# Expert rows gathered up to sixteen blocks ahead, row and result stores on ScalarE's queue, and a second product two blocks behind, in a two-layer mixer with routed experts

## The chip, the core and the metric

The kernel runs on one core of a Trainium2 chip. The metric is the device time of one execution in microseconds; the median of three runs of the kernel before is 674.62 us (672.95 to 680.81). Durations below come from one execution that was profiled. In the profile, PE is TensorE's matmul, PEld its weight load, DVE is VectorE, ACT is ScalarE, POOL is GpSimd and SP is SyncE; an instruction is named by its line in the kernel (L543), and tiles by the program's names.

## What is computed

The input x has 8 sequences of 256 tokens with 128 channels. Two layers follow each other, each a token mixer and a feed-forward part with eight experts of width 512, of which each token uses two:

```python
x = x + ga * mixer(layernorm(x) * (1 + ca) + sa)
x = x + gb * experts(layernorm(x) * (1 + cb) + sb)
```

The vectors sa, ca, ga, sb, cb, gb come from a small modulation product for each sequence. Layer 0's mixer is a retention with 16 heads of 8 channels, a decay mask, a normalisation for each head and a gate; layer 1's is softmax attention with a causal mask inside chunks of 256. The experts are `relu(x W1 + b1) W2 + b2` in layer 0 and `(silu(x G) * (x U)) D` in layer 1; each token's two experts are the two largest router logits, weighted by a softmax over these two.

## The kernel before

**Tiling.** The 2048 tokens are four groups of 512 (two sequences each), and a half is two groups, 1024 tokens. The mixers work through groups and sequences; the experts work through halves.

**Experts as sorted rows.** `route` (L382) makes the router logits of a half, takes the two best experts of each token, and gives each of the 2048 (token, expert) pairs a slot so that each expert's slots form whole blocks of 128. A half has NS = 23 blocks. The modulated tokens (tile hm, made by POOL) are stored to DRAM as xs (L401). A product of one-hot tiles (hot, L512) with owner tiles, the matmul pown (L520), gives the token list: token number for each slot (L529).

`gather` (L535, DMA at L543) brings the 128 rows of one block from xs into one quarter of a row tile xr; a row tile holds NTL = 4 blocks, and there are three. `begun` (L548) issues the first eight gathers of the first half of a layer and reports after the fourth that the layer can begin. `experts` (L556) loops over the 23 blocks: `matrices` (L574) has SP read the block's expert number and load its weights (six buffers); `hidden0` or `hidden1` makes the first product from xT, the transposed rows (`turn`, L563); `leave` (L588) makes the second product py (L591) of the block before, copies it to yr, and `store` (L599) sends four blocks at a time to ys in DRAM on ACT's queue. `combined` (L634) then gathers both results of each token from ys (yk, L659), weights and adds them, and adds them to x with `add_gated` (L346), on POOL except for the last half. In layer 1 the finished x is stored to the output (L1192).

**Order.** The order on each engine is the order in which the program writes the instructions; nothing is reordered. Work that isn't in the loop at hand is written as generators, the side jobs, kept in a list. `tick` (L171) moves each of them by one step, `ticks(step)` does so several times at a place in a loop, and `hop(step)` inside a job makes it pause for several ticks. PACE (L41) gives these numbers, 1 where a step isn't named. `settle` (L186) runs side jobs to their end with no loop beside them. The stages are: retention with the routing of layer 0 beside it, until the first gathers are written (L1173); experts of half 0 and of half 1 of layer 0, with layer 1's modulation, the combination of half 0 and the opening of the attention beside them (`Attention.opening`, L1100); attention with the routing of layer 1; experts of both halves of layer 1, with the combination of half 0 beside the second; the combination of half 1 alone at the end (L1197).

**Queues.** Gathers of both kinds, row stores (L401) and half 0's output stores are DMAs on POOL's queue, between POOL's own work (rstd, hm, masks, placing, adding x). Weights go on SP's queue, ys stores on ACT's.

Of the kernel before, what the change touches and what calls it, by code (L numbers as in the profile page):

```python
# [10 lines left out]
FP = mybir.dt.float32  # L11
BF = mybir.dt.bfloat16
# [6 lines left out]
P = 128  # L19
# [13 lines left out]
W0 = 2 * FF + NFC  # L33
NSC = 7
# [6 lines left out]
PACE = {  # L41
    "a0.kt": 3, "a0.rstd": 3, "a0.xn": 2, "a1.k": 2, "a1.q": 2, "a1.rstd": 2, "a1.stats": 2,
    "a1.turn": 2, "a1.xn": 0, "att.sums": 2, "att.weights": 0, "c0.b2": 2, "c0.begin": 2,
    "c0.gw": 3, "c1.begin": 8, "c1.gather": 0, "c1.scale": 4, "cl.begin": 3, "cl.pp": 0,
    "head3": 0, "n.pp": 0, "n.q": 2, "n.rstd": 2, "op.max": 2, "op.place": 0, "r0.both": 2,
    "r0.rstd": 4, "r1.rstd": 2, "ret.scores": 2, "ret.sums": 2,
}
# [3 lines left out]
def kernel(  # L51
# [239 lines left out]
    def modulated_norm(key, g, layer, shift, scale, got, hm=None):  # L291


        st = sm.tile([P, NTL, 6], FP, tag="lnst", name=f"lnst_{key}")
# [87 lines left out]
    def route(layer, half, ready, wr, bias):  # L382
# [10 lines left out]
        for u in range(HG):  # L393
            g = HG * half + u
            while g not in ready:
# [5 lines left out]
            nc.gpsimd.dma_start(  # L401
                out=xs[half].rearrange("(u t p) c -> u p t c", p=P, t=NTL)[u], in_=hm
            )
# [7 lines left out]
            yield from hop(f"r{layer}.logits")  # L411
            if bias is None:
                nc.vector.tensor_copy(lg[:, tiles, :], pv)
            else:
                nc.vector.tensor_tensor(
                    lg[:, tiles, :], pv, bias.unsqueeze(1).to_broadcast([P, NTL, NE]), ALU.add
                )
# [4 lines left out]
        at = sm.tile([P, 2, HT], FP, tag="at", name=f"at_{key}")  # L422
# [33 lines left out]
        need = sm.tile([P, NE], FP, tag="need", name=f"need_{key}")  # L456
        nc.vector.tensor_reduce(need, big, AX.X, ALU.add)
        nc.vector.tensor_tensor(big, upto, need.unsqueeze(1).to_broadcast([P, NE, NE]), ALU.mult)
        ends = sm.tile([P, NE], FP, tag="ends", name=f"ends_{key}")
        nc.vector.tensor_reduce(ends, big, AX.X, ALU.add)  # L460
        first = sm.tile([P, NE], FP, tag="first", name=f"first_{key}")
# [11 lines left out]
        slot_f = sm.tile([P, 2, HT], FP, tag="slf", name=f"slf_{key}")  # L473
# [4 lines left out]
        row = sm.tile([P, 2, HT], I32, tag="row", name=f"row_{key}")  # L478
# [29 lines left out]
        for t in range(HT + 2):  # L508
            if t < HT:
                for k in range(2):  # L510
                    hot = sm.tile([P, P], BF, tag="hot", name=f"hot_{key}_{k}_{t}", bufs=8)
                    nc.vector.tensor_scalar(  # L512
                        hot, row16, part[:, 1, k, t : t + 1], None, ALU.is_equal
                    )
                    hots.append(hot)
# [17 lines left out]
    raw, begin = {}, set()  # L533

    def gather(layer, half, j):  # L535

        q, t = j // NTL, j % NTL
        if t == 0:
            raw[layer, half, q] = wk.tile(
                [P, NTL, P], FP, tag="xr", name=f"xr_{layer}_{half}_{q}", bufs=3  # L540
            )
        token = routed[layer, half][4]
        nc.gpsimd.indirect_dma_start(  # L543
# [12 lines left out]
    def experts(layer, half, blob, hidden, following=None):  # L556
# [48 lines left out]
        last = None  # L605
        ahead = [(layer, half, j) for j in range(2 * NTL, NS)]
        if following:
            ahead += [(*following, j) for j in range(2 * NTL)]
        total = len(ahead)
        for j in range(NS):  # L610
            q = j // NTL
            for _ in range(2):
                if ahead and ahead[0][:2] in routed and total - len(ahead) <= j:
                    gather(*ahead.pop(0))
# [6 lines left out]
            if last is not None:  # L621
                leave(*last)
# [3 lines left out]
            last = (j, w2, h, yr)  # L626
        leave(*last)
# [6 lines left out]
    def combined(layer, half, finished, add=nc.gpsimd):  # L634
# [16 lines left out]
        for at in range(HT + 2):  # L651
# [43 lines left out]
            add_gated(f"{key}_{u}", g, gates, 1, acc, acc, add)  # L695
            finished(g)
# [19 lines left out]
    def retention(groups, finished):  # L716
# [93 lines left out]
        def normed(g, n):  # L810
# [4 lines left out]
            if n == 0:  # L815
                gn[g] = (
                    sm.tile([P, 2, 6], FP, tag="gnst", name=f"gnst_{key}"),
# [94 lines left out]
    class Attention:  # L912
# [58 lines left out]
        def maxima(self, at, c, k):  # L971
# [29 lines left out]
            if k == c:  # L1001
# [6 lines left out]
                rest = sm.tile([P, 4, 4], FP, tag="nrest", name=f"nr_{tag}")  # L1008
# [151 lines left out]
    with tc.manual_schedule():  # L1160
# [34 lines left out]
        sides.append(combined(1, 0, leaves(nc.gpsimd)))  # L1195
# [101 lines left out]
```

## Time and profile before

| | us |
|---|---|
| median of three runs | 674.62 |
| the profiled execution, whole | 674.16 |
| its span, first to last instruction | 672.5 |
| PE busy | 522.9 (78%) |
| DVE busy | 359.7 (53%) |
| POOL busy | 326.0 (48%) |
| ACT busy | 234.5 (35%) |
| row gathers, L543, 92 of them | 88.5, mean 0.962 |
| result gathers, L659, 64 of them | 61.5, mean 0.960 |

From the timelines, the stages begin and end at about these times: retention until 121, experts of layer 0 from 134 to 205 and from 206 to 296, attention from 299 to 479, experts of layer 1 from 483 to 566 and from 568 to 641, the last combination until 672.

Busy is time in which an engine works on an instruction of its own; waiting for a semaphore and issuing DMAs are not in it, except that a GpSimd DMA's row counts the time in which POOL makes the DMA. "Idle before" is the time an engine stood before the instructions of a group, and the name after the arrow is what ended most of it; "issue" stands for time in which the profile shows nothing that was waited for. A matmul in float32 shows as two records. The granted clock is TensorE's, as a share of full speed.

### The profile page before, as it was taken

The page shows a single profiled execution, that of the slowest core. Times are in us where ns is not written, and L with a number is a line of the kernel's source. Part 1 is how long each engine was busy: PE and PEld are TensorE (multiplying, and loading weights), DVE is VectorE, ACT ScalarE, POOL GpSimd, SP SyncE. Part 2 cuts the span into 40 slices and gives each one's busy share as a digit, 9 for nine tenths or more (in the row PEclk, how much of TensorE's full clock was granted, in tenths as well). Part 3 has the DMA queues.
Part 4 walks back from the last instruction along what each step waited for, and adds up shares of the span by engine and source line. Part 5 has one row for each costly group of instructions (what it writes and reads, how often), then busy time and mean ns, then how long its engine had stood idle before and what let it go on. Part 6 is the DMA issues. An engine that isn't in the chain of part 4 may idle for free.

```text
span 672.5 us, 13020 instructions
## 1 busy us (share of the span) xinstructions
PE 522.9 (78%) x4672; PEld 400.6 (60%) x4672; DVE 359.7 (53%) x1137; ACT 234.5 (35%) x517; POOL 326.0 (48%) x458
## 2 busy tenths in 40 slices
PE   4798885596778588987888888588797799889910
PEld 4555453386777487663454444345697798789910
DVE  3668879374533245646588667956153632223422
ACT  2453442233123244364555545234423122123310
POOL 4466682676243435317667427146446042613364
PEclk9999796799777799998799999979899899899965
DMA  6000002458666257500100000010698699689412
GB/s 185 25 1 1 18 1 86 151 169 204 212 203 207 94 182 204 182 28 18 31 18 17 2 1 17 7 39 21 195 342 196 244 280 315 227 281 311 170 58 63
DMA packets 43087, 84.13 MB, mean 125 GB/s; under 512 B 6472, under 2 KB 21456, under 8 KB 43024
## 3 DMA queue, kind: packets, MB, share of 16 engines
q1 hardware_dynamic: 25072, 64.42, 28.3%
q0 software_dynamic: 5792, 12.86, 8.6%
q10 hardware_dynamic: 12160, 6.03, 3.0%
q8 instruction: 37, 0.61, 0.4%
q14 instruction: 26, 0.21, 0.1%
HBM read 74.11 MB, written 9.18 MB: 124 GB/s over the span
## 4 chain that ended last, share of the span: by engine, by line
PE 36%; DVE 12%; issue 8%; POOL 5%; ACT 3%; another core or an unknown queue 2%; DMA 1%; POOLq 0%; ACTq 0%; DVEq 0%
PE py L591 7%; PE pg L1150 5%; DVE nm L995 5%; PE pu L1150 4%; PE sm L989 4%; PE ph L892 3%; POOL yk_c L659 3%; PE se L1042 2%; PE sm L981 2%; PE yd L1067 1%; PE pn L1084 1%; DMA yk_c<-ys,slot_r 1%; PE pz L1020 1%; ACT e L1048 1%
## 5 line engine op out<-in xcount | busy, mean ns | idle before, releaser
L543 POOL DMA_INDIRECT xr<-xs,token_r x92 | 88.5, 962 | 92.9 <-PE pt_s L281 26.3
L659 POOL DMA_INDIRECT yk_c<-ys,slot_r x64 | 61.5, 960 | 55.1 <-issue 35.7
L995 DVE TENSOR_REDUCE nm<-sm 128x4 f32<-128x512 f32 x96 | 59.5, 681 | 39.2 <-PE sm L989 39.2
L1157 DVE TENSOR_TENSOR h<-pu,sg 128x512 f32<-128x512 f32 x46 | 31.7, 690 | 88.8 <-PE pu L1150 46.6
L1048 ACT ACTIVATE e<-se 128x512 f32<-128x512 f32 x96 | 49.7, 603 | 47.4 <-PE se L1042 37.0
L892 PE MATMUL ph<-xT,we 128*128 128x128 f32 x368 | 55.7, 299 | 10.9 <-ACT xT L569 9.3
L591 PE MATMUL py<-we,h 128*128 128x128 f32 x368 | 54.4, 293 | 7.4 <-issue 5.0
L359 POOL TENSOR_SCALAR_AFFINE_SELECT e<-e 128x512 f32<-128x512 f32 x64 | 38.4, 633 | 43.2 <-ACT e L1048 43.0
L892 PEld LDWEIGHTS ph<-xT,we 128*128 128x128 f32 x368 | 50.9, 213 | 11.3 <-ACT xT L569 10.1
L1150 PE MATMUL pg<-xT,we 128*128 128x128 f32 x368 | 52.6, 287 | 6.3 <-ACT xT L569 4.3
L591 PEld LDWEIGHTS py<-we,h 128*128 128x128 f32 x368 | 49.5, 206 | 12.1 <-issue 7.0
L1155 ACT ACTIVATE sg<-pg 128x512 f32<-128x512 f32 x46 | 27.4, 597 | 81.4 <-PE pg L1150 54.7
L591 PE MATMUL py<-wd,h 128*128 128x128 f32 x368 | 50.3, 278 | 3.8 <-issue 2.0
L1150 PE MATMUL pu<-xT,we 128*128 128x128 f32 x368 | 50.3, 279 | 3.7 <-issue 3.7
L900 DVE TENSOR_SCALAR h<-ph,we 128x128 f32<-128x128 f32 x92 | 27.9, 344 | 47.1 <-PE ph L892 20.6
L1150 PEld LDWEIGHTS pg<-xT,we 128*128 128x128 f32 x368 | 47.5, 201 | 8.8 <-ACT xT L569 4.8
L898 ACT ACTIVATE h<-ph,we 128x128 f32<-128x128 f32 x92 | 28.7, 364 | 60.9 <-issue 29.2
L1150 PEld LDWEIGHTS pu<-xT,we 128*128 128x128 f32 x368 | 46.8, 197 | 3.8 <-issue 3.8
L591 PEld LDWEIGHTS py<-wd,h 128*128 128x128 f32 x368 | 44.9, 192 | 4.5 <-DVE h L1157 2.4
L595 DVE COPY yr<-py 128x128 f32<-128x128 f32 x92 | 26.4, 287 | 34.4 <-PE py L591 12.2
L989 PE MATMUL sm<-kz,qs_a 32*128 32x512 f32 x192 | 34.3, 721 | 0.0
L569 ACT COPY xT<-pt_s 128x512 f32<-128x512 f32 (+1 forms) x24 | 13.6, 567 | 55.6 <-PE pt_s L281 42.6
(221 smaller groups left out, 982.6 us busy)
## 6 DMA issues: line engine op xcount, KB each, us to landing
we<-in_l_ew_dram SPq DMA_DIRECT2D x46, 514.0 KB
we<-in_l_ew_dram SPq DMA_DIRECT2D x46, 512.0 KB
wd<-in_l_ew_dram SPq DMA_DIRECT2D x46, 256.0 KB
ys<-yr ACTq DMA_DIRECT2D x20, 256.0 KB
xs<-hm_r POOLq DMA_DIRECT2D x8, 256.0 KB
xr<-xs,token_r POOLq DMA_INDIRECT x92
x<-in_x_in_dram SPq DMA_DIRECT2D x4, 256.0 KB
yk_c<-ys,slot_r POOLq DMA_INDIRECT x64
```

What stands on the lines that cost most here:

```text
L359: nc.gpsimd.affine_select(out=src, in_=src, compare_op=ALU.is_ge, fill=0.0, base=0, pattern=[[0, 4], [1, P]], channel_multiplier=-1,)
L543: nc.gpsimd.indirect_dma_start(out=raw[layer, half, q][:, t, :], out_offset=None, in_=xs[half][:, :], in_offset=bass.IndirectOffsetOnAxis( ...
L591: nc.tensor.matmul(py, lhsT=h[:, fc, :], rhs=w2[:, fc * C : (fc + 1) * C], start=(fc == 0), stop=(fc == NFC - 1),)
L659: nc.gpsimd.indirect_dma_start(out=yk[:, k, :], out_offset=None, in_=ys[half][:, :], in_offset=bass.IndirectOffsetOnAxis(ap=slot[:, k, at ...
L892: nc.tensor.matmul(ph[:, i, :], lhsT=we[:, fc * P : (fc + 1) * P], rhs=xT, start=True, stop=True)
L898: nc.scalar.activation(h[:, fc, :], ph[:, i, :], AF.Relu, bias=b1)
L900: nc.vector.tensor_scalar(h[:, fc, :], ph[:, i, :], b1, 0.0, ALU.add, ALU.max)
L989: nc.tensor.matmul(scs[i], lhsT=qs[part, t0 : t0 + P], rhs=kz[part, :, k * P : (k + 1) * P], start=(k != c), stop=True,)
L995: nc.vector.tensor_reduce(nm[:, 4 * i : 4 * i + 4], scs[i], AX.X, ALU.max, negate=True)
L1048: nc.scalar.activation(e, scs[i], AF.Exp)
L1150: nc.tensor.matmul(p[:, fc, :], lhsT=we[:, i * FF + fc * P : i * FF + (fc + 1) * P], rhs=xT, start=True, stop=True,)
L1157: nc.vector.tensor_tensor(h, pu, sg, ALU.mult)
```

## The change

Six things are changed.

- Gathers: `experts` writes up to two gathers for each block, one ahead of the first product and one after the second product. A rule on row tiles replaces the count: a gather is written if its row tile is less than four row tiles ahead of the one in use. There are four row tiles xr in place of three, and 16 blocks of the following half are gathered in the loop of the half before, in place of 8. `begun` still writes eight.
- The row store of xs moves from POOL's queue, ahead of the logits, to ACT's, after the pause at the logits.
- The output stores of half 0 move from POOL's queue to ACT's, and a pause named c1.out stands ahead of them.
- With e1.behind at 2, layer 1's second product is written two blocks behind the first.
- PACE has other numbers for a good part of the steps.
- Small tiles have fewer buffers (3 to 2, hot 8 to 4).

```diff
+AHEAD = 16
 PACE = {
-    "a0.kt": 3, "a0.rstd": 3, "a0.xn": 2, "a1.k": 2, "a1.q": 2, "a1.rstd": 2, "a1.stats": 2,
-    "a1.turn": 2, "a1.xn": 0, "att.sums": 2, "att.weights": 0, "c0.b2": 2, "c0.begin": 2,
-    "c0.gw": 3, "c1.begin": 8, "c1.gather": 0, "c1.scale": 4, "cl.begin": 3, "cl.pp": 0,
-    "head3": 0, "n.pp": 0, "n.q": 2, "n.rstd": 2, "op.max": 2, "op.place": 0, "r0.both": 2,
-    "r0.rstd": 4, "r1.rstd": 2, "ret.scores": 2, "ret.sums": 2,
+    "a0.kt": 3, "a0.rstd": 3, "a0.xn": 2, "a1.hT": 2, "a1.k": 2, "a1.q": 3, "a1.rstd": 2,
+    "a1.stats": 0, "a1.turn": 2, "a1.xn": 0, "att.sums": 2, "att.weights": 0, "blanks": 2,
+    "c0.begin": 2, "c0.gw": 3, "c1.begin": 8, "c1.gather": 2, "c1.out": 3, "c1.scale": 2,
+    "cl.begin": 4, "cl.pp": 0, "e1.behind": 2, "head10": 0, "head13": 2, "head3": 0, "head9": 0,
+    "mod.rows": 2, "n.pp": 0, "n.q": 2, "n.rstd": 2, "op.first": 4, "op.max": 3, "op.place": 0,
+    "op.project": 0, "r0.count": 0, "r0.hot": 0, "r0.logits": 0, "r0.rstd": 4, "r0.top": 0,
+    "r0.xn": 0, "r1.count": 0, "r1.logits": 0, "r1.rstd": 4, "ret.scores": 2, "ret.sums": 2,
 }
...
-            nc.gpsimd.dma_start(
-                out=xs[half].rearrange("(u t p) c -> u p t c", p=P, t=NTL)[u], in_=hm
-            )
...
             yield from hop(f"r{layer}.logits")
+            nc.scalar.dma_start(
+                out=xs[half].rearrange("(u t p) c -> u p t c", p=P, t=NTL)[u], in_=hm
+            )
...
-                    hot = sm.tile([P, P], BF, tag="hot", name=f"hot_{key}_{k}_{t}", bufs=8)
+                    hot = sm.tile([P, P], BF, tag="hot", name=f"hot_{key}_{k}_{t}", bufs=4)
...
-                [P, NTL, P], FP, tag="xr", name=f"xr_{layer}_{half}_{q}", bufs=3
+                [P, NTL, P], FP, tag="xr", name=f"xr_{layer}_{half}_{q}", bufs=AHEAD // NTL
             )
         token = routed[layer, half][4]
+        gathered[layer, half] = j + 1
...
-        last = None
-        ahead = [(layer, half, j) for j in range(2 * NTL, NS)]
+        hiddens = []
+        ahead = [(layer, half, j) for j in range(gathered[layer, half], NS)]
         if following:
-            ahead += [(*following, j) for j in range(2 * NTL)]
-        total = len(ahead)
+            ahead += [(*following, j) for j in range(AHEAD)]
+
+        def onward(j):
+
+            if ahead and ahead[0][:2] in routed:
+                part, at = ahead[0][1:]
+                if at // NTL + (part - half) * -(-NS // NTL) < j // NTL + AHEAD // NTL:
+                    gather(*ahead.pop(0))
+
         for j in range(NS):
             q = j // NTL
-            for _ in range(2):
-                if ahead and ahead[0][:2] in routed and total - len(ahead) <= j:
-                    gather(*ahead.pop(0))
+            onward(j)
...
             store()
-            if last is not None:
-                leave(*last)
+            if len(hiddens) == PACE.get(f"e{layer}.behind", 1):
+                leave(*hiddens.pop(0))
+            onward(j)
             ticks(f"e{layer}.leave")
...
-            last = (j, w2, h, yr)
-        leave(*last)
+            hiddens.append((j, w2, h, yr))
+        for more in hiddens:
+            leave(*more)
         store()
...
             add_gated(f"{key}_{u}", g, gates, 1, acc, acc, add)
+            if layer == 1:
+                yield from hop("c1.out")
             finished(g)
...
-        sides.append(combined(1, 0, leaves(nc.gpsimd)))
+        sides.append(combined(1, 0, leaves(nc.scalar)))
```

## The prediction

> **What bounds it now.** I read the slices of the page first, then windows around every hole of TensorE, then the timelines of the engines in the holes, then the groups of the lines that the diff touches. The slices (16.8 us each) of the page:
>
> ```profile
> PE   4798885596778588987888888588797799889910
> DVE  3668879374533245646588667956153632223422
> POOL 4466682676243435317667427146446042613364
> ```
>
> TensorE (PE) is busy 78% of the span. No engine is full throughout, so what counts is TensorE's holes: the hand-over from layer 0's mixer to its experts (slice 7), holes inside the expert loops, and the tail (the last two slices). The windows of three of these (columns: length, then busy us and count of PE, weight loads, DVE, ACT, POOL, then granted clock, DMA share, GB/s):
>
> ```profile
> 96.00:122.00 26.00, 17.89 (x206) 11.26 (x206) 21.19 (x91) 7.28 (x15) 10.85 (x17) 0.74 0.35 118
> 126.00:134.00 8.00, 2.45 (x11) 1.29 (x11) 0.00 (x0) 0.58 (x1) 6.65 (x9) 0.58 0.26 66
> 212.00:231.00 19.00, 11.31 (x66) 10.40 (x65) 6.44 (x18) 3.98 (x13) 11.48 (x12) 0.77 0.32 99
> ```
>
> VectorE (DVE) limits the end of the mixer, 21.2 of 26 us, and then does nothing for 8 us. Why, the two timelines say:
>
> ```profile
> 121.75 0.18 DVE L529 SCALAR_TENSOR_TENSOR token_r<-pown_r,low_r 128x23 int32<-128x23 f32 x1
> ...
> 136.08 0.61 DVE L900 TENSOR_SCALAR h<-ph,we 128x128 f32<-128x128 f32 x2 [10.12 <-PE ph L892]
> ```
> ```profile
> 129.59 0.48 PE L281 MATMUL pt_s<-ident,xr 128*128 128x128 f32 x1 [2.38 <-DMA xr<-xs,token_r]
> 131.90 0.48 PE L281 MATMUL pt_s<-ident,xr 128*128 128x128 f32 x1 [1.83 <-DMA xr<-xs,token_r]
> 132.82 0.48 PE L281 MATMUL pt_s<-ident,xr 128*128 128x128 f32 x1 [0.44 <-DMA xr<-xs,token_r]
> 133.97 0.58 PE L892 MATMUL ph<-xT,we 128*128 128x128 f32 x1 [0.68 <-ACT xT L569]
> ```
>
> The token list is ready at 121.9, four gathers follow, and the first expert matmul runs at 134.0. These four gathers are the only ones TensorE ever waits for; so more rows ahead, by itself, removes no wait of TensorE. In layer 1 the token list (447.4) comes 35 us before the first expert matmul (482.7), so nothing is to be had there. The tail, on GpSimd (POOL):
>
> ```profile
> 642.34 1.25 POOL L355 TENSOR_TENSOR x<-x,acc_c 128x512 f32<-128x512 f32 x1 [10.52 <-DVE acc_c L352]
> 643.89 0.81 POOL L1192 DMA_DIRECT2D out_dram<-x  x1 [0.29 <-POOL x L355]
> 645.00 0.99 POOL L659 DMA_INDIRECT yk_c<-ys,slot_r  x1 [0.30 <-issue]
> ```
>
> Sixteen such gathers, 1.25 us apart, carry the last 27 us, and a store stands ahead of them. The gathers' group on the page, and what the second product waits for (view of L591, 482 to 641):
>
> ```profile
> L543 POOL DMA_INDIRECT xr<-xs,token_r x92 | 88.5, 962 | 92.9 <-PE pt_s L281 26.3
> ```
> ```profile
>   DVE h L1157: 4.2, 6
> ```
>
> **The skill.** The Trainium skill, "DMA: Bandwidth & Descriptors", section "Issuing engines are not separate DMA queues", says that the issuing engine changes only the sequencer time spent on the issue. The trace bears this out as far as it shows: a 256 KB store keeps POOL 0.81 to 0.86 us (plus 0.3 before it) and ScalarE's (ACT's) queue 0.37. "Perfetto Trace Analysis", "Summary: the profiler window per engine type", says that a GpSimd DMA's interval is the making of descriptors, not the transfer. It agrees: the first gather ran at 124.2 for 1.1 us, and its row tile was used at 126.9. "TensorE: Matmul & The Clock Gate", "What's actually happening", says that an idle stretch of about 3.4 us halves the clock. It agrees: clock 0.58 in 126 to 134, and 0.58 us for the first ph against a median of 0.275. So a removed hole is worth a little more than its length.
>
> **Part by part.**
>
> *Routing of layer 0 in fewer steps.* A tick moves each side job by one step; the mixer gives 64 ticks (8 rows, 2 halves, 2+2). Group 1 is finished at tick 44. From there, the steps put the fourth gather at tick 71 now: the mixer ends at 64, so seven ticks are spent in the waiting loop. With xn, logits, top, count and hot at 0 and both at 1, it is tick 60. From logits (100.9, tick 55) to token (121.7, tick 67) one tick takes 1.73 us, so 11 ticks would be 19 us; DVE can't give that. Between 99 and 122 routing takes 13.3 us of it and other work 10.6, which is all there is. I take: logits at 98, routing's 13.3, 3.5 of other work let in between (0.7 per tick, five ticks), 1.5 for two round trips to PE: token at 116, six earlier. Four gathers at 1.25, 2.3 to land, 1.2 for turn and xT, 1.5 for other POOL work: first matmul at 126, against 134. **-8** (-11 if POOL is free; 0 if the displaced mixer work ends as much later).
>
> *Gathers two per block, 16 ahead, four row buffers.* 92 gathers stay 92. Eight more per layer move from the second half's loop into the first half's. On POOL's queue they stand ahead of rstd, hm and x: two per block take 2.5 us against a block's 1.79 on PE (16 records of 0.112), so rstd of group 3 can be late by some 3 us, with DVE's xn, then h, then PE behind it. **+2** (0 to +5). In the second halves the yk gathers and x come sooner; nothing waits there that I can price, 0. What the bursts do to other engines is in the rivals.
>
> *Eight row stores and two result stores to ACT.* POOL loses 10 x 1.15 = 11.5 us; on the path lies the one at 643.89: the last ys packets landed at 643.1, so the gathers can start at 643.9. **-1.1**. ACT gains 10 x 0.37, idle time in the holes. But each row store waits for hm from POOL with ACT's next activations behind it. Held against now, ACT would be free at plg's end and hm ready at most 0.8 us later, in seven of eight cases. At 467.8 ACT would wait until 473.0, because POOL had gathers and masks before hm; behind it are four exp (470.6), then yd on PE. **+2** (0 to +5.2; r1.rstd's two further ticks may move it). SP's queue carries weights only and is not passed.
>
> *Second product two behind.* PE waits 4.2 us for h before L591 in layer 1, as shown; with one more block between (2.68 us) most goes, and the first product is late next, by buffers of weights held one block longer. **-3** (-4 to +1). The last two products come after the loop, no more work.
>
> *Attention's opening.* op.first, op.max, op.project add four ticks; a1.stats takes two back ahead of the statistics of group 1. Two ticks are one block, 1.8 us. PE has only 0.2 us of idle between 294.7 and 299.3: this chain just fits now. **+1.8** (0 to +3.6).
>
> *Buffers of small tiles.* hot from 8 to 4: row tile t reuses what the matmul of t-2 reads, so DVE waits for PE inside routing. No such wait is in the trace; one routing has eight row tiles, the bound is 0 to 3 us each, four times. **+2**, half a microsecond each. The tiles from 3 to 2 are read by DVE itself or a step later, 0. The other steps (head, modulation, closings, c1, blanks) move work under loops in which PE is 80 to 90% busy: 0, give or take 3.
>
> *c1.gather 2, c1.scale 2.* The last x of half 0 stays at tick 48 of 46 in the loop, so still after it: 0.
>
> Sum: -8 +2 -1.1 +2 -3 +1.8 +2 = -4.3. The hole at 126 also costs a half-clock stretch (6.8 us at 0.5, as the clock in the trace shows), 3.4 us of work that goes with it: -7.7, say -8. The profiled execution's own time is 674.2 (span 672.5 and 1.7 around), 0.5 below the median: **666 us**.
>
> **Rivals.**
>
> *Slower: bursts of gathers stall the other engines.* In 212 to 231, twelve gathers run back to back and PE loses 7.7 us, with ACT and DVE late for no reason the trace names (6.2 us "issue" on ACT): 0.64 us a gather. Bursts of eight at 156 to 165, 180 to 190 and 507 to 517 stand beside holes as well. For: first halves now get 31 gathers each, in longer runs. Against: eight in a row at 537 to 547 cost 1 us. If all 62 paid 0.64, 40 us, less the 9 such holes cost there now: +31, with -8 it is 697. It decides from 22 us of new holes upwards. Chance 0.14.
>
> *Clearly faster: the second halves lose their holes.* They have eight gathers less to run beside the 16 yk. Holes there now: 13.2 us in 204 to 295 (7.7, 2.3, 1.4, 1.0, 0.8), 4 in 566 to 641. With those gone, 666 - 14 = 652. Against: yk stays. Chance 0.28.
>
> *No change: DVE stays the bound.* The routing pulled ahead pushes the mixer's last masks back by as much; the gathers further ahead were never waited for. -8 falls away: 674. Chance 0.20. The main case has 0.38.
>
> **Numbers.** Over 2% means below 661 or above 688, about what a measurement here can tell from no change. Main case 660 to 672, mostly within; faster is the second rival and a little of the main case, 0.33; within 0.53; slower 0.14. The range 648 to 688 takes in the faster rival and leaves most of the slower one out.
>
> **To be seen after.** The first ph near 126 and DVE's hole before it gone; the first tail gather at 643.9 relative to the last py (3.2 us after it instead of 4.3); "DVE h" before L591 under 1.5 us; hm stores in ACT's queue, with a gap ahead of exp. Wrong if ph still starts 12 us after token with token unmoved, or if holes beside gather bursts grow in the first halves.

## The result, and the profile after

The changed kernel takes 682.08 us in the median of 20 runs (675.26 to 687.93), the kernel before 674.74 in the same session (20 runs). The ratio is 1.0089, 95% interval 1.006 to 1.0118: about 0.9% slower, where 1.3% faster was forecast. The profiled execution takes 677.33 us, with a span of 675.6, 3.1 us longer than the span before. It lies 4.8 us below the median of its kernel, so the two traces show 3.1 us of the 7.3 between the medians.

The slices of the changed kernel's page, 16.9 us each:

```profile
PE   4798785797787697987798897688698979589910
DVE  3667767457434245547778668956167323133422
POOL 4466570875434435017847336338552422702354
```

The hole of the hand-over (slice 7, counted from 0, a 5 before) is filled to 7, but slice 6 is a 5 as before and slice 4 (68 to 84 us, beside the routing of group 0) has gone from 8 to 7. The windows over the end of the mixer show the exchange (columns as in the prediction):

```profile
96.00:122.00 26.00, 18.01 (x147) 10.57 (x151) 17.00 (x77) 7.88 (x14) 8.99 (x16) 0.66 0.25 77
126.00:134.00 8.00, 4.34 (x78) 3.05 (x75) 2.93 (x13) 2.19 (x5) 7.00 (x9) 1.00 0.20 43
```

In the 26 us that were VectorE's, it now works 17.0 us and not 21.2. Mixer work that was not reached there fills a part of 126 to 134. The timelines show what each engine waited for. TensorE:

```profile
96.97 0.90 PE L284 MATMUL pt_r<-ident,xn_r 128*128 128x128 f32 x3 [2.17 <-DVE xn_r L309]
...
104.45 0.24 PE L441 MATMUL pc_r<-both_r,before 128*128 128x72 bf16 x1 [2.64 <-DVE both_r L434]
...
115.40 2.66 PE L523 MATMUL pown_r<-owner_r,hot_r 128*128 128x46 bf16 x16 [4.18 <-DVE hot_r L515]
...
129.99 1.06 PE L813 MATMUL pr<-a,vz 128*32 128x128 f32 x26 [0.17 <-POOL a L362]
130.98 0.66 PE L284 MATMUL pt_s<-ident,xr 128*128 128x128 f32 x4
133.55 1.16 PE L905 MATMUL ph<-xT,we 128*128 128x128 f32 x8 [1.92 <-ACT xT L573]
```

VectorE:

```profile
101.85 0.19 DVE L416 COPY lg_r<-plg_r 128x32 f32<-128x32 f32 x1 [3.85 <-PE plg_r L408]
...
108.91 1.29 DVE L791 TENSOR_TENSOR a<-rs,tri 128x512 f32<-128x512 f32 x2 [1.62 <-PE rs L783]
...
118.31 0.18 DVE L532 SCALAR_TENSOR_TENSOR token_r<-pown_r,low_r 128x23 int32<-128x23 f32 x1
...
120.48 1.29 DVE L791 TENSOR_TENSOR a<-rs,tri 128x512 f32<-128x512 f32 x2 [1.84 <-PE rs L783]
```

In the kernel before, the longest wait of TensorE here is the same one, and VectorE finds the logits (lg) finished when it comes to them:

```profile
115.75 0.22 PE L520 MATMUL pown_r<-owner_r,hot_r 128*128 128x46 bf16 x1 [4.41 <-DVE hot_r L512]
```
```profile
100.87 0.18 DVE L413 COPY lg_r<-plg_r 128x32 f32<-128x32 f32 x1
```

So TensorE's waits are not what grew: from 94 to 122 us it waits 9.0 us for VectorE at xn, both and hot, and before it waited 9.1 at xn, lg, both, o_a and hot; its idle time in the window is 8.0 us against 8.1. What grew is VectorE's idle time, 9.0 us in place of 4.8. It waits 3.9 us for plg and 1.6 and 1.8 for rs (before: none for plg, 1.8 for one rs and 1.7 for pown). The rs are the mixer's products that stand behind the routing's matmuls in TensorE's order and so come after TensorE's own waits for VectorE. A routing written in one piece is a chain that goes back and forth between two engines that keep the order of the program, and at each turn one of them stands. TensorE's granted clock is lower as well, 0.66 in place of 0.74: in 18 us of work it gets through 147 matmul records and not 206, not all of the same kinds.

The lateness does not begin in this window. Of the mixer's 16 products pr<-a, the eighth starts at 71.8 us where it started at 67.0, beside the routing of group 0; the twelfth at 98.9 and not 93.1; the fourteenth at 121.1 and not 104.5; the last at 129.2 and not 120.0. The token list is ready at 118.3, 3.4 us earlier; the mixer's last product ends at 131.0, 9.7 us later; the first expert transposes follow at once and wait for no gather; the first ph runs at 133.55, against 133.97.

The tail on GpSimd has no store in it any more:

```profile
646.42 1.26 POOL L358 TENSOR_TENSOR x<-x,acc_c 128x512 f32<-128x512 f32 x1 [12.47 <-DVE acc_c L355]
648.44 0.97 POOL L670 DMA_INDIRECT yk_c<-ys,slot_r  x1 [0.75 <-issue]
```

All stages, in us, as their limits stand in the traces. The first pair is the session of the result. The second pair is from a later session on another chip, on which the kernel before takes 626.11 us (PE's idle time in brackets):

| stage | before | after | before, second chip | after, second chip |
|---|---|---|---|---|
| to the mixer's last product | 121.3 (27.5) | 131.0 (31.8) | 118.6 (26.7) | 133.2 (33.5) |
| to the first ph | 12.7 | 2.5 | 12.8 | 1.3 |
| layer 0, first half | 72.0 (16.0) | 75.7 (13.5) | 58.7 (6.1) | 67.1 (10.8) |
| layer 0, second half | 90.3 (18.0) | 85.4 (13.0) | 77.8 (7.5) | 74.2 (5.4) |
| to the attention | 3.0 | 5.3 | 3.0 | 5.3 |
| attention | 179.6 | 175.8 | 175.7 | 180.3 |
| to layer 1's experts | 3.9 | 6.0 | 1.3 | 1.3 |
| layer 1, first half | 84.9 (10.3) | 86.6 (10.1) | 77.5 (5.5) | 74.4 (3.8) |
| layer 1, second half | 73.4 (5.2) | 76.7 (8.7) | 64.2 (0.0) | 64.0 (0.0) |
| tail | 31.5 | 30.5 | 31.5 | 30.7 |

The 12.7 us between mixer and experts were not empty: TensorE worked 5.3 us of them, in products that close the mixer and begin the second half's routing. Of the 2.5 us after, it works 0.6; the rest of that work now stands in the first half of the experts.

One profile of a stage is good to a few us: the mixer of the kernel before ended at 121.3 us in one profile and at 118.6 in the other.

### The profile page after: what moved, and what is told of

It reads as the page before. It is cut to its first block, busy times and chain, and to the rows that moved or that the text cites. A ratio compares the mean times of both kernels' runs of the same rounds, so it can differ in the third digit from the quotient of the medians.

```text
span 675.6 us, 13089 instructions
## 1 busy us (share of the span) xinstructions
PE 528.6 (78%) x4672; PEld 404.1 (60%) x4672; DVE 362.4 (54%) x1137; ACT 234.7 (35%) x517; POOL 319.3 (47%) x448
## 4 chain that ended last, share of the span: by engine, by line
PE 37%; DVE 12%; issue 11%; POOL 6%; ACT 2%; DMA 1%; ACTq 0%; POOLq 0%; DVEq 0%
PE py L595 6%; PE pg L1163 5%; PE pu L1163 5%; DVE nm L1008 4%; PE sm L1002 4%; POOL yk_c L670 3%; PE sm L994 2%; PE yd L1080 2%; PE ph L905 2%; PE se L1055 2%; PE pn L1097 1%; DMA yk_c<-ys,slot_r 1%; POOL xr L547 1%; POOL e L362 1%; PE pt_s L284 1%
## 5 line engine op out<-in xcount | busy, mean ns | idle before, releaser
L1170 DVE TENSOR_TENSOR h<-pu,sg 128x512 f32<-128x512 f32 x46 | 31.8, 690 | 85.3 <-PE pu L1163 48.9
L1163 PE MATMUL pg<-xT,we 128*128 128x128 f32 x368 | 54.1, 286 | 14.5 <-issue 13.3
L595 PE MATMUL py<-we,h 128*128 128x128 f32 x368 | 55.8, 297 | 4.9 <-DVE h L913 2.7
L595 PEld LDWEIGHTS py<-we,h 128*128 128x128 f32 x368 | 50.6, 208 | 8.4 <-DVE h L913 3.4
L595 PE MATMUL py<-wd,h 128*128 128x128 f32 x368 | 50.5, 282 | 3.2 <-issue 3.1
L595 PEld LDWEIGHTS py<-wd,h 128*128 128x128 f32 x368 | 46.5, 197 | 3.6 <-issue 3.6
L795 ACT COPY a<-rs 128x512 f32<-128x512 f32 x32 | 17.2, 590 | 45.6 <-PE rs L783 34.4
L1002 PE MATMUL sm<-kz,qs_a 32*128 32x512 f32 x192 | 32.6, 722 | 0.0
```

What stands on the lines that cost most here:

```text
L595: nc.tensor.matmul(py, lhsT=h[:, fc, :], rhs=w2[:, fc * C : (fc + 1) * C], start=(fc == 0), stop=(fc == NFC - 1),)
L1002: nc.tensor.matmul(scs[i], lhsT=qs[part, t0 : t0 + P], rhs=kz[part, :, k * P : (k + 1) * P], start=(k != c), stop=True,)
L1163: nc.tensor.matmul(p[:, fc, :], lhsT=we[:, i * FF + fc * P : i * FF + (fc + 1) * P], rhs=xT, start=True, stop=True,)
L1170: nc.vector.tensor_tensor(h, pu, sg, ALU.mult)
```

## The experiments

Five sessions, each with runs of the kernel before on its own chip: 625.8 us (first four kernels), 626.1 (next four), 675.5 (four), 628.0 (four) and 684.5 (last two). Ratios are to these.

### Steps or structure

`pace_only`: the kernel before with the changed kernel's step table (without e1.behind and c1.out, which it has no place for): the three groups of steps that are later tried apart (`r0_pace_only`, `head_steps`, `late_steps`).

```diff
-    "a1.q": 2, "a1.stats": 2, "c0.b2": 2, "c1.gather": 0, "c1.scale": 4, "cl.begin": 3,
-    "op.max": 2, "r0.both": 2, "r1.rstd": 2,
+    "r0.count": 0, "r0.hot": 0, "r0.logits": 0, "r0.top": 0, "r0.xn": 0,
+    "head9": 0, "head10": 0, "head13": 2, "mod.rows": 2, "blanks": 2,
+    "a1.hT": 2, "a1.q": 3, "a1.stats": 0, "c1.gather": 2, "c1.scale": 2, "cl.begin": 4,
+    "op.first": 4, "op.max": 3, "op.project": 0, "r1.count": 0, "r1.logits": 0, "r1.rstd": 4,
```

> The kernel before with all numbers of PACE of the changed kernel, and nothing else (gathers, stores, second product, buffers as before). Lump theory (layer 0's routing, written in five steps in place of twelve, makes TensorE wait in order inside the mixer, and the other steps are worth little): the mixer ends near 131 us instead of 121, the first expert matmul stays at 133 to 136, and the time is as the changed kernel's, ratio 1.005 to 1.015. Structure theory (the row gathers, stores and buffers cost the time): ratio 0.985 to 1.002.

`structure_only`: the changed kernel with that edit undone, and `"e1.behind": 2, "c1.out": 3` kept.

> The changed kernel with PACE of the kernel before, except e1.behind 2 and c1.out 3, so gathers 16 ahead, stores on ScalarE, second product two behind and the smaller buffers are all in. Lump theory: mixer ends at 121, first expert matmul at 132 to 134, ratio 0.985 to 1.0. Structure theory: ratio 1.008 to 1.02, with longer expert stages.

`r0_pace_only`: the kernel before, with layer 0's routing steps alone.

```diff
-    "r0.both": 2,
+    "r0.count": 0, "r0.hot": 0, "r0.logits": 0, "r0.top": 0, "r0.xn": 0,
```

> The kernel before with only the steps of layer 0's routing of the changed kernel (r0.xn, logits, top, count, hot 0 and both 1). Lump theory: mixer ends at 128 to 132, token list at 116 to 119, first expert matmul at 132 to 135, and the first half of layer 0 no shorter; ratio 1.0 to 1.01. If the prediction's first term was right and something else ate it: first expert matmul near 126, ratio 0.985 to 0.995.

`after_old_r0`: the changed kernel with the reverse of that edit.

> The changed kernel with the steps of layer 0's routing as before (r0.both 2, the others 1) and all else changed. Lump theory: mixer ends near 121, first expert matmul 132 to 134, ratio to before 0.995 to 1.003, so below the changed kernel's 1.009. Structure theory: stays at 1.006 to 1.012.

Measured: pace_only 1.0057 (1.0026 to 1.0088), structure_only 1.0149 (1.0101 to 1.0196), r0_pace_only 1.0047 (1.0017 to 1.0076), after_old_r0 1.0139 (1.009 to 1.0188). The routing's steps alone move the picture as in the changed kernel (hand-over 1.3 us, mixer's end at 131.6 us, first ph at 132.9) and lose 0.5%, some 3 us of 626. So the part that was to bring 8 us costs 3. Beside before_again (below; another chip, of the same speed) the mixer ends 13.0 us later, the hand-over is 11.5 us shorter, and the first half of layer 0 is 4.4 us longer, 63.1 against 58.7, of which only 0.7 us is idle time of TensorE. The rest is work; in the hand-over, where TensorE worked 6.4 us, it now works 0.6. after_old_r0 met neither of its expectations. The two kernels with the new structure and the old routing steps lost more than the changed kernel itself, which their parts could not explain; a part of that was cleared up later, below.

### The gathers and the stores

`before_again` and `after_again`: both kernels as they are, on this chip.

> The kernel before, unchanged, for a profile beside those of the experiments. If the holes that the first profile shows beside bursts of gathers come from the program (the prediction's slower rival), they must be here too: 7 to 10 us idle in the second half of layer 0 between 212 and 231, 90 us for that stage. If they come from outside the program, the stage takes 74 to 80 us, as in the experiments before this one, and the span is near 624.

> The changed kernel, unchanged. If the parts add up (numbers of PACE 1.0057, everything else 1.0149 less overlap), ratio 1.008 to 1.02; mixer ends at 131 to 134, second half of layer 1 at 64 us without idle time.

`ahead_only`: the kernel before with the gather rule, four row tiles and the smaller buffers.

```diff
-                [P, NTL, P], FP, tag="xr", name=f"xr_{layer}_{half}_{q}", bufs=3
+                [P, NTL, P], FP, tag="xr", name=f"xr_{layer}_{half}_{q}", bufs=AHEAD // NTL
...
-        ahead = [(layer, half, j) for j in range(2 * NTL, NS)]
+        ahead = [(layer, half, j) for j in range(gathered[layer, half], NS)]
         if following:
-            ahead += [(*following, j) for j in range(2 * NTL)]
+            ahead += [(*following, j) for j in range(AHEAD)]
```

> The kernel before with only the gathers changed (two per block, 16 ahead, four row tiles) and the smaller buffers that make room for them; stores on POOL, second product one behind, old PACE. Theory that POOL's gathers hold up the routing of the second half: x of group 3 (142 in the first profile) at 148 to 152, the second token list 4 to 8 us late, first half of layer 0 longer by as much, ratio 1.008 to 1.016. Rival, stores on ScalarE or the second product cost the time: ratio 0.997 to 1.003.

`stores_on_act`: the kernel before with both stores on ScalarE's queue and the pause c1.out. The row store keeps its old place, ahead of the logits.

```diff
-            nc.gpsimd.dma_start(
+            nc.scalar.dma_start(
                 out=xs[half].rearrange("(u t p) c -> u p t c", p=P, t=NTL)[u], in_=hm
             )
...
-        sides.append(combined(1, 0, leaves(nc.gpsimd)))
+        sides.append(combined(1, 0, leaves(nc.scalar)))
```

> The kernel before with only the stores moved to ScalarE's queue (with c1.out 3). Theory that the gathers are the cost: ratio 0.996 to 1.001, the tail 1 us shorter, and first gather of the tail 3.2 us after the last product. Rival, ScalarE blocked behind hm: 1.004 to 1.012 with ACT idle ahead of exp near the end of the attention.

Measured: before_again 622.71 us in its one run; after_again 1.0117 (1.0066 to 1.0169); ahead_only 1.017 (1.0115 to 1.0225); stores_on_act 1.0006 (0.9961 to 1.0051), its tail 31.0 us against 31.5. The stores do nothing that can be told. The gathers looked like the whole loss, with layer 0's first half at 69.3 us against 58.7. GpSimd's timeline of ahead_only and the group of its gathers say otherwise:

```profile
138.57 0.94 POOL L539 DMA_INDIRECT xr<-xs,token_r  x1 [2.72 <-DMA xr<-xs,token_r]
139.82 0.95 POOL L539 DMA_INDIRECT xr<-xs,token_r  x1 [0.30 <-issue]
143.20 0.95 POOL L539 DMA_INDIRECT xr<-xs,token_r  x1 [2.44 <-DMA xr<-xs,token_r]
144.45 0.94 POOL L539 DMA_INDIRECT xr<-xs,token_r  x1 [0.30 <-issue]
147.54 0.94 POOL L539 DMA_INDIRECT xr<-xs,token_r  x1 [2.15 <-DMA xr<-xs,token_r]
148.51 1.27 POOL L350 TENSOR_TENSOR x<-x,res_a 128x512 f32<-128x512 f32 x1
```
```profile
L539 POOL DMA_INDIRECT xr<-xs,token_r x96 | 92.6, 964 | 77.1 <-PE pg L1155 20.7 <-issue 20.1 <-PE ph L897 10.9
```

A gather that waits for a gather to land, and 96 of them where the program needs 92. With the old steps the experts' loop begins when four of `begun`'s eight gathers are written. The new rule then starts its list at the fifth, and `begun`, still at work, writes five to eight as well. Each pair writes the same rows, so the second waits until the first has landed. In the changed kernel all eight are written before the loop begins, and it has 92. The same doubles are in structure_only and after_old_r0: these three ratios are those of kernels with four gathers and some 7 us of waits that neither original has.

### The gathers without the doubles

`ahead_once` and `structure_once`: ahead_only and structure_only, each with

```diff
-        ahead = [(layer, half, j) for j in range(gathered[layer, half], NS)]
+        ahead = [(layer, half, j) for j in range(max(gathered[layer, half], 2 * NTL), NS)]
```

> The gather part alone again (two per block, up to sixteen blocks ahead, four row tiles, the smaller buffers; stores on POOL, second product one behind, old steps), with one difference: its list begins at the ninth gather at the earliest. In the run before it held 96 gathers where the kernel before holds 92: with the old steps the experts begin when four of the first eight gathers have been issued, and the list then began at the fifth, so that gathers five to eight were made twice, and three of them waited 2.7, 2.4 and 2.2 us for the first copy to land. Theory of the double gathers: those 7.3 us and 4 x 1.25 us made the loss, so 92 gathers, none waiting for a landing, x of group 3 added at 141 to 143 (148.5 with the doubles, 139.4 before), layer 0's first half 60 to 63 us (69.3, 58.7), ratio 0.998 to 1.005. Theory of the rate: gathers at two a block push group 3's work back in any case, so x at 146 or later, the half 66 us or more, ratio 1.010 or more.

> Everything of the change but the step table (the table of the kernel before with second product two behind and three steps at c1.out), with the list of gathers beginning at the ninth at the earliest, so 92 gathers and not 96. Theory of the double gathers: 60 to 63 us in layer 0's first half (69.2 with the doubles), tail near 31, ratio 0.996 to 1.003, since stores and second product cost nothing. Theory of the rate: 66 us or more, ratio 1.009 or more (1.0149 with the doubles).

`after_old_gather`: the changed kernel with the rule of before, three row tiles and eight gathers ahead included; the loop's part of the edit:

```diff
-            onward(j)
+            for _ in range(2):
+                if ahead and ahead[0][:2] in routed and total - len(ahead) <= j:
+                    gather(*ahead.pop(0))
```

> The changed kernel whole, with the gather rule of before (two tries at the start of a block, no more gathers than blocks, from the ninth on, eight of the next half; three row tiles). Here both kernels have 92 gathers and none is made twice. In the changed kernel 18 gathers lie ahead of the addition of group 3's x at 153.1 us, and layer 0's first half takes 67.1 us. Theory of the rate: with the old rule some four gathers (4 x 1.25 = 5 us) go behind that addition: x at 147 to 149, the half 62 to 64 us, ratio 1.003 to 1.007, so about 0.006 of the changed kernel's 1.0117 are the gathers'. Theory of the step table: the loss is the lumped routing and the head's steps alone; the half stays above 66 us and the ratio at 1.010 or more.

`behind_only`: the kernel before with e1.behind 2 and, in the loop,

```diff
...
-            if last is not None:
-                leave(*last)
+            if len(hiddens) == PACE.get(f"e{layer}.behind", 1):
+                leave(*hiddens.pop(0))
...
```

> The kernel before with layer 1's second product two blocks behind and nothing else. Theory of the prediction: 3 us less in layer 1's first half (77.5 to 74.5), ratio 0.993 to 0.997. Rival: PE has no hole that this fills on this chip (layer 1's second half shows no idle PE at all), so the half stays at 77 to 78 us and the ratio at 0.998 to 1.002.

Measured: ahead_once 1.0018 (0.9988 to 1.0047), structure_once 1.0112 (1.006 to 1.0164, six runs), after_old_gather 1.0095 (1.0055 to 1.0135), behind_only 1.0039 (1.0009 to 1.007). In ahead_once the waits are gone, and the mixer's result of group 3 is added to x at 141.38 us, in the kernel before at 141.99:

```profile
138.34 0.95 POOL L539 DMA_INDIRECT xr<-xs,token_r  x1 [0.30 <-issue]
141.38 1.26 POOL L350 TENSOR_TENSOR x<-x,res_a 128x512 f32<-128x512 f32 x1 [2.09 <-DVE res_a L347]
```
```profile
L539 POOL DMA_INDIRECT xr<-xs,token_r x92 | 89.0, 967 | 86.5 <-issue 21.5 <-PE pg L1155 20.4 <-PE pt_s L276 20.2
```

Counted from the first ph, that is 10.5 us and not 8.0, so the gathers do put this addition back, by 2.5 us. So the theory of the double gathers holds for ahead_only, and the gather rule by itself changes the time by nothing that can be told. (This chip was a slow one; the lengths of halves in the expectation were those of the chip before and do not apply.) The theory of the rate has half a point: with the old rule in the changed kernel the first half of layer 0 is 68.7 us instead of 75.7, the second 89.7 instead of 85.4, and the ratio stays at 1.0095 (on another chip of the same speed) against 1.0089. The rule moves time from one half to the other. structure_once lies where the theory of the rate put it, though the gathers alone (ahead_once) cost nothing that can be told. Its parts give 1.0018 x 1.0039 x 1.0006, or 1.0063, just inside the lower end of its interval; that difference stays open.

### Where the steps lose and gain, and the second product

`late_steps`: the kernel before with all changed steps but r0, head, blanks and mod.rows.

```diff
-    "a1.q": 2, "a1.stats": 2, "c0.b2": 2, "c1.gather": 0, "c1.scale": 4, "cl.begin": 3,
-    "op.max": 2, "r1.rstd": 2,
+    "a1.hT": 2, "a1.q": 3, "a1.stats": 0, "c1.gather": 2, "c1.scale": 2, "cl.begin": 4,
+    "op.first": 4, "op.max": 3, "op.project": 0, "r1.count": 0, "r1.logits": 0, "r1.rstd": 4,
```

`head_steps`: the kernel before with

```diff
+    "head9": 0, "head10": 0, "head13": 2, "mod.rows": 2, "blanks": 2,
```

`after_behind1`: the changed kernel with

```diff
-"e1.behind": 2,
+"e1.behind": 1,
```

`late_all`: the changed kernel with the old steps for r0, head, blanks and mod.rows, e1.behind 1, and the list of gathers from the ninth on.

> The kernel before with every changed step but those of the routing of layer 0, the head, the blanks and the rows of the modulation (so a1, c0, c1, cl, op and r1 as in the changed kernel). Theory that routing and head are the loss: layer 0's second half and layer 1's first half are 2 to 4 us shorter each, as in the run with the whole table (74.2 against 77.8, 75.7 against 77.5), the opening of the attention 2.3 us longer, so -2 to -5 us, ratio 0.992 to 0.998. Rival, that the other steps carry no gain of their own and the shorter halves there were only work that the lumps had done earlier: 0.999 to 1.004.

> The kernel before with the five steps of the head alone (head9 and head10 0, head13, mod.rows and blanks 2). In the changed kernel with the old routing steps the mixer's end lay 4.7 us later (126.2 against 121.5). Theory that these steps cost it: mixer's end 4 to 5 us later than in the kernel before on the same chip, first product of layer 0's experts as much later, ratio 1.004 to 1.008. Rival, that the head is free and the 4.7 us were another step's or the scatter of one profile: ratio 0.998 to 1.002.

> The changed kernel whole, with layer 1's second product one block behind as before. Theory that two behind costs by itself (1.0039 alone): ratio 1.004 to 1.008, layer 1's second half 2 to 4 us shorter than in the changed kernel where that took 76.7. Theory of the prediction (two behind saves 3 us): ratio 1.012 to 1.017, layer 1's first half longer. If it does nothing: 1.009 to 1.012.

> The changed kernel without its losing parts: stores on ScalarE's queue, gathers two per block and sixteen ahead from the ninth on, smaller buffers, the later stages' steps of the changed kernel; the routing of layer 0, the head, blanks and rows as before, second product one behind. If the losses are where the runs so far put them, the parts add up to late_steps times the gathers' 1.0018 times the stores' 1.0006 (tail 1 us shorter): 0.993 to 0.999. If the parts do not add up (structure without steps gave 1.0112 where its parts gave 1.0063): 1.003 or more.

Measured: late_steps 0.9936 (0.9907 to 0.9965), head_steps 1.0029 (0.9998 to 1.0061), after_behind1 1.0161 (1.0102 to 1.022, six runs), late_all 0.9964 (0.9936 to 0.9991). The later stages' steps gain 0.6%, and this is the best version of the study; in late_all layer 0's second half takes 74.4 us and layer 1's first 73.5 (before_again: 77.8 and 77.5). The head's steps lie between the two expectations, and their interval just takes in no change; VectorE waits 2.6 us once for GpSimd's cleared tiles (vz) in them, which it does not in the kernel before, and the mixer ends at 122.7 us (before_again: 118.6). after_behind1 went against behind_only: its ratio lies where the prediction's theory put it, but its interval overlaps after_again's, and layer 1's first half, which was to be longer, is not (the halves take 73.6 and 64.2 us, in after_again 74.4 and 64.0), so nothing was shown there.

late_all is the changed kernel without three of its parts, the routing's steps, the head's steps and the second product two behind, and without the doubles. These three parts hold its whole loss: 1.0117 with them (after_again), 0.9964 without, on two chips of nearly the same speed. Gathers, stores and small buffers are in both.

`late_best`: stores_on_act with these steps; `late_best_behind2`: the same with the edit of behind_only and e1.behind 2.

```diff
-    "a1.stats": 2, "c0.b2": 2, "c1.gather": 0, "c1.scale": 4, "cl.begin": 3, "r1.rstd": 2,
+    "a1.hT": 2, "a1.stats": 0, "c1.gather": 2, "c1.scale": 2, "cl.begin": 4,
+    "r1.count": 0, "r1.logits": 0, "r1.rstd": 4,
```

> The kernel before with both stores on ScalarE's queue and the changed steps of a1 (but a1.q), c0, c1, cl and r1; old gathers, old steps of head, routing of layer 0, projection (op) and a1.q, second product one behind. If the longer attention comes from a1.q and the projection's steps: opening 3.0 us, attention 175 to 176, layer 0's second half and layer 1's first half still 2 to 4 us short, tail 1 us shorter, ratio 0.984 to 0.991. If the shorter half and the longer attention are the same work moved: the second half is long again (77 to 78 us) and the ratio 0.993 to 0.998.

> late_best with layer 1's second product two blocks behind, and nothing else. Theory of the prediction: 3 us less, so 0.004 to 0.005 below late_best on the same chip. Theory that it costs: 0.003 to 0.005 above late_best. If it does nothing: within 0.002 of late_best, layer 1's halves within 1 us in the profiles.

Measured: late_best 0.998 (0.9954 to 1.0007), late_best_behind2 1.0034 (1.001 to 1.0057). Without a1.q and op the attention opens after 0.8 us, not 3.0; but the two halves that these steps shortened elsewhere are long (91.8 and 91.2 us). The ratio is at the upper edge of the second expectation; the lengths in both were those of a faster chip, and the kernel before has no profile on this one, so which of the two holds is open. The pair differs in one thing on one chip: 1.0034/0.998 is 1.0054, with the two half-widths taken together as independent some 0.0036, so two blocks behind costs some 1.2 to 6 us there. It lies where it was to gain. The second half of layer 1 in late_best, in late_best_behind2, and in before_again on the faster chip:

```profile
573.00:647.00 74.00, 68.27 (x571) 66.11 (x571) 23.97 (x54) 18.65 (x36) 26.77 (x28) 0.98 0.76 238
```
```profile
578.70:657.60 78.90, 69.23 (x571) 67.64 (x571) 24.07 (x54) 18.79 (x36) 26.83 (x28) 0.91 0.70 223
```
```profile
525.30:589.50 64.20, 64.17 (x571) 63.84 (x571) 24.15 (x54) 18.87 (x36) 26.91 (x29) 1.00 0.80 278
```

The same 571 matmul records: on the faster chip TensorE is never idle in this half, so there is nothing to gain. On the slower one it idles 5.7 us with one behind and 9.7 with two, at a lower clock. (The second of these executions took 689.98 us, 5.2 above the median of its kernel.) The other profiles on slower chips agree: idle 5.2 us in before and 4.3 in ahead_once, with one behind; 8.7, 7.5, 8.6 and 9.4 in after, structure_once, after_old_gather and behind_only, with two. What TensorE waits for ahead of the second product from 480 us on, in late_best and in late_best_behind2 (total us, times, longest):

```profile
PE py L585 <- DVE h L1153: 4.4, 6, 1.9
```
```profile
PE py L585 <- issue: 7.3, 12, 1.1
```

The wait for h is gone, as intended, and 7.3 us for which the trace names nothing stand in its place; ahead of the first products (pg, pu) such time is 6.8 us in the one and 5.0 in the other. No wait for weights is named among them.

The trace does show where that time lies. In late_best_behind2 the whole idle time of the second half, 9.7 us, falls between 589 and 605 us, where TensorE runs single matmuls up to 1.4 us apart:

```profile
589.00:605.00 16.00, 6.33 (x26) 4.91 (x25) 0.98 (x2) 1.17 (x2) 9.46 (x10) 0.68 0.36 109
```
```profile
597.23 0.37 PE L585 MATMUL py<-wd,h 128*128 128x128 f32 x1 [0.83 <-issue]
598.66 0.55 PE L585 MATMUL py<-wd,h 128*128 128x128 f32 x1 [1.06 <-issue]
```

GpSimd makes 15 gathers there, row and result gathers in turn, 1.25 us apart and without a pause, from 583.0 to 601.4. In late_best it makes the same 15 with a pause of 2.1 us after the seventh, and most of the 5.7 us of idle time lie in these two stretches; on the faster chip 16 in a row leave TensorE no idle time at all (before_again):

```profile
576.10:585.00 8.90, 6.97 (x59) 6.44 (x58) 1.14 (x3) 1.16 (x2) 6.61 (x7) 1.00 0.72 223
586.60:597.00 10.40, 8.55 (x55) 7.68 (x55) 1.58 (x3) 1.49 (x3) 7.54 (x8) 0.85 0.80 254
```
```profile
529.90:550.00 20.10, 20.10 (x183) 20.10 (x182) 7.18 (x16) 5.64 (x10) 15.11 (x16) 1.00 0.98 352
```

All five profiles with two behind on slower chips have 14 or 15 gathers in one run here, the three with one behind have two runs of seven or eight. So the cost stands beside the longer run of gathers. Whether the gathers make TensorE stand, and whether the order of the second product makes the run longer, no run tests.

## Why the prediction was wrong

**The step that failed** is the first, "Routing of layer 0 in fewer steps", -8. Its sum goes from the token list over four gathers to the first expert matmul (token at 116, matmul at 126) and puts the mixer work that the routing displaces at nothing: of VectorE's 10.6 us of other work it lets in 3.5, and the other 7.1 were to run later at no cost. Measured: token at 118.3, the mixer's last product at 131.0 in place of 121.3, the first ph at 133.55 in place of 133.97; and alone these steps cost 0.47%, +3 us (r0_pace_only). The chain itself was not priced too low: 16.6 us from the logits' copy to the token list, against the 18 that were allowed. But the copy came at 101.85 and not at 98, because TensorE had a mixer product to do ahead of plg (98.9 to 100.8), and the first ph stands behind the mixer's last product in TensorE's order, whatever the gathers do. Nor was the hand-over an empty hole: 5.3 of its 12.7 us were work, which had to go elsewhere.

The prediction had this in a bracket ("0 if the displaced mixer work ends as much later") and as its rival of no change. That rival was right that the mixer is pushed back, by more than "as much"; its reason, that VectorE stays the bound, was not, for VectorE is idle 9.0 of the 26 us and not 4.8. That the turns between the two engines take this time is read from the timelines; no run changes them alone. The half-clock stretch's 3.4 us fell with it: the clock at 126 to 134 did rise from 0.58 to 1.00, but that of 96 to 122 went from 0.74 to 0.66.

**Second product two behind**, -3 (to +1). The intended wait went: ahead of the second product of layer 1 (L595 in the changed kernel) TensorE no longer waits for h. But the wait was smaller than was read. The view of the line, with its 4.2 us and 6 times, counts a wait at the weight load and again at the matmul. The list of waits has them apart, and TensorE's matmuls waited 1.8 us, 3 times, so -3 was more than this wait had to give:

```profile
PE py L591 <- DVE h L1157: 1.8, 3, 1.0
```

And the time without a named cause grew, in the view of the line (which counts it twice as well) from 3.6 to 6.7 us. Alone it cost +2.6 us (behind_only, 0.0039 of 676) and +3.7 us (0.0054 of 681), both on slower chips; on the faster ones nothing could be told. The sign was wrong. That the weights' buffers came "late next" is not shown; what the traces show beside the lost time is the longer run of gathers.

**Gathers**, +2 (0 to +5), and **small buffers**, +2: together +1.2 us (ahead_once, 0.0018 of 675; -0.8 to +3.2). The delay that was described is there: alone, group 3's x comes 2.5 us later after the first ph, and under the lumped routing 19.6 us after it with the new rule and 14.1 with the old (after, after_old_gather). But what the first half loses by it the second gets back.

**Stores**: tail -1.0 where -1.1 was said. The +2 for a blocked ScalarE hardly showed: at 471.18 the store was issued, and the exp behind it ran at 471.59, 0.3 us after the last of its products (se), where the prediction had ScalarE waiting until 473.0. All told 1.0006.

**Attention's opening** +1.8: 5.3 against 3.0 us, +2.3. Right.

**The other steps**, "0, give or take 3", hid two terms of opposite sign: the head's steps +1.8 us (0.0029 of 628, an interval that just takes in nothing), the later ones -4.0, the longer opening included.

**The sum from the runs**, as ratios: routing 1.0047, head 1.0029, later steps 0.9936, gathers 1.0018, stores 1.0006, second product 1.0039 make 1.0075 when multiplied, against 1.0089 and 1.0117. The terms come from different chips and have 0.003 to 0.0045 each, so the sum agrees and proves no more than that.

**The rivals.** Bursts of gathers do not stall the engines as a property of the program: the same kernel with the same bursts has no idle TensorE in layer 1's second half on the faster chip. On the slower chips idle time does stand beside them, so this rival saw something real, at a smaller size: the holes in the first halves, where it looked for them, did not grow (16.0 and 10.3 us before, 13.5 and 10.1 after); that of layer 1's second half did, from 5.2 to 8.7. The other rival, that second halves lose holes, came true in layer 0 alone, by 5.0 us of PE's 18.0; with the old rule in the changed kernel 12.8 us remained, so it was not the gathers that had left.

## What to carry to other kernels

An engine that is busy 80% before a hole is not thereby the bound, and a hole is not empty because its digit is low; before pulling a dependent chain forward, ask what stands between its steps now and what stands in the hole, because that work is what will be late. A wait that is shown in the kernel after proves little until the same wait is looked up in the kernel before. A rule that reads the state of the program while it is being written (which gather comes next) holds for the step table that it was tuned with; count instructions in every recombination before its time is believed. A table changed as a whole hides gains: here 0.6% in some steps lay under losses in others.

## What was not expected of the hardware

The same program ran in 626 to 628 us on three chips and in 675 to 685 on the others, with the same order of instructions. The spans 621.0 and 672.5 differ mostly in the expert halves (58.7 against 72.0 us in layer 0's first), where the granted clock was 0.93 against 0.88 and TensorE idle 6.1 against 16.0 us; the attention, with little DMA traffic, took 175.7 against 179.6. What makes the difference between the chips was not tried. In layer 1's second half a run of 15 gathers stands beside 9.7 us of idle time of TensorE on a slower chip (late_best_behind2), and one of 16 beside none on a faster (before_again). The sign of edits that fill TensorE's holes may depend on the chip, which is not shown, for the runs differ in more than the chip: layer 1's first half was 73.5 us in late_all on a faster chip against 77.5 before, and 91.2 in late_best on a slower one, at a clock of 0.90, against 84.9 in the kernel before in the first session.
